# Attention fills: the score products of two slots issued together, in turns over four strips of 32 rows

## The chip, the core and the metric

One core of a Trainium2 chip runs the whole program. TensorE (PE) multiplies, VectorE (DVE) and ScalarE (ACT) read its results from PSUM, GpSimd (POOL) masks and issues indirect DMAs, SyncE (SP) issues the other DMAs. The metric is the device time of the kernel in microseconds, the median of several runs. Everything is float32; the profile shows each float32 product as two passes on PE (two weight loads and two matmuls).

## The reference

The input x has 8 batches of 512 rows and 128 columns. Three blocks follow one another: half a feed-forward block with a top-2 mixture of 8 experts, causal attention with 16 heads of 8 columns, and the same feed-forward block again. Only attention is touched here:

```
q = (x @ q_w + q_b)  -> 16 heads of 8 columns          k, v likewise from kv_w
att = q @ k.T / sqrt(8) + slope[h] * (key - query)     (512 x 512 for each batch and head)
att = where(key <= query, att, -inf); att = softmax(att)
y = att @ v, heads joined, @ o_w + o_b
x = x + y            (x here is layer-normalised on the way in)
```

## The kernel before

Attention works in **units**: one batch b and a group g of 4 heads, so 8 x 4 = 32 units. The four heads of a unit lie in four strips of 32 partitions (rows 32j to 32j+31) of the tiles `qs` and `ks`, and head j of a product uses strip j of PE's rows alone. A strip holds the head's 8 columns and some constant rows for the position term and the causal mask. One row of `qs` (`R_MAX`) holds, for each query, the maximum of its scores.

Each unit makes every score twice.

- `fill_a` makes scores with the queries on the partitions (`sa`). DVE reads them (line 925) and keeps the maximum of each query in `mx`. A unit has 12 fills f: f // 4 picks a pack of query tiles, `PACKS_A`, and f % 4 the head. The packs make products of 128 and 256 columns, of 384, and of 512.
- `maxima` transposes `mx` on PE (`pm`), copies it with ACT (`mr`) and sends it with four DMAs on SP's queue into the rows `R_MAX` of `qs`, one DMA for each head.
- `fill_b` makes the scores again with the keys on the partitions (`sb`), now with the maximum taken off by the row `R_MAX`. ACT takes the exponential into `pr` (line 964), and on each fourth fill POOL sets the masked corner of four heads to zero (line 969). Its packs make products of 512 columns, of 384, and of 256 and 128. The head is (f + 2) % 4.
- `weigh` multiplies the probabilities with v (`py`, three parts), `leave` copies the sum with ACT, `divide` transposes it on PE (`pyt`) and DVE divides by the sum of the row.

Time is cut into **slots**. Slot s issues one fill of each pass: `fill_a` number s and `fill_b` number s - LAG, where LAG is 20. With s % 4 = c the first uses strip c and the second strip (c + 2) % 4. Fills of `sa` have three PSUM buffers (`ps_a`), those of `sb` three others (`ps_b`), and everything else two (`ps_x`, tag "misc").

Behind the fills of a slot stand its **tasks**, from the dictionary `todo`. With r for the slot within a unit of 12 slots, the tasks that use PE are: r = 1 `py` part 1, r = 2 `pm`, r = 4 `py` part 2 and `leave`, r = 6 `pyt`, r = 10 `py` part 0. Once in a batch come, for the batch after or before: in the second unit `turn` (`apt`, r = 11); in the third `spread` (`pp`, r = 3 and 5), `turn_back` (`pyT`, r = 8), `project` (`apo`, r = 9), `f_stats` (r = 10, on DVE and ACT) and `values` (`pv`, r = 11); in the fourth `f_turn` (`pt`, r = 3), `f_half` (r = 5, ACT) and `f_logits` (`pl`, r = 6). In the first two batches the tasks also fetch and mix what the experts of the block before made, and after the fourth batch `f_sort` and `f_send` sort rows for the block after.

Matrix products, transposes and some POOL and ACT instructions keep the order in which the program issues them (`mm`, `tp`, `pin`). The others are ordered for each engine by a planner, which goes by data, by program order and by its own times. [...]

The loop that sets the order of a slot is this:

```
            for s in range(max(todo) + 1):
                if 0 <= s < UNITS * FILLS:
                    fill_a(*divmod(s, FILLS))
                if 0 <= s - LAG < UNITS * FILLS:
                    fill_b(*divmod(s - LAG, FILLS))
                for f, args in todo.get(s, ()):
                    f(*args)
```

Of the kernel before, what the change touches and what calls it, by code (L numbers as in the profile page):

```python
# [56 lines left out]
def tile_macaron(  # L57
# [125 lines left out]
    def mm(*args, **kw):  # L183
        pin(T.matmul(*args, **kw))  # L184
# [699 lines left out]
    def attention():  # L884
# [4 lines left out]
        with ExitStack() as ph:  # L889
# [13 lines left out]
            FILLS = 3 * GH  # L903
            LAG = FILLS + 8
            UNITS = NB * NG


            def fill_a(u, f):
                b, g = divmod(u, NG)
                pack, j = PACKS_A[f // GH], f % GH  # L910
                if f == 0:
                    mxs[u] = two.tile([P, GH, TT], F32, name=f"mx{u}", tag="mx")
                q, k, r = qs[b % 2], ks[b % 2], slice(32 * j, 32 * j + 32)
                sa = ps_a.tile([P, S], F32, name=f"sa{u}_{f}", tag="sa")
                at = 0
                for i in pack:
                    n = (i + 1) * P
                    mm(
                        sa[:, at : at + n], q[r, g, i * P : n], k[r, g, :n], start=True, stop=True
                    )  # L920
                    at += n
                at = 0
                for i in pack:
                    n = (i + 1) * P
                    V.tensor_tensor_reduce(  # L925
                        junk[:, :n], sa[:, at : at + n], mask_q[:, S - n :],
                        1.0, -3.0e38, ALU.add, ALU.max, mxs[u][:, j, i : i + 1],
                    )
                    at += n
# [16 lines left out]
            def fill_b(u, f):  # L946
                b, g = divmod(u, NG)
                p, j = f // GH, (f + 2) % GH
                pack = PACKS_B[p]
                width = sum(S - kt * P for kt in pack)  # L950
                if f % GH == 0:
                    prs[u, p] = prob.tile([P, GH, width], F32, name=f"pr{u}_{p}", tag=f"pr{p}")
                pr = prs[u, p]
                q, k, r = qs[b % 2], ks[b % 2], slice(32 * j, 32 * j + 32)
                sb = ps_b.tile([P, S], F32, name=f"sb{u}_{f}", tag="sb")
                at = 0
                for kt in pack:
                    n = S - kt * P
                    mm(
                        sb[:, at : at + n], k[r, g, kt * P : (kt + 1) * P], q[r, g, kt * P :],  # L960
                        start=True, stop=True,
                    )
                    at += n
                A.activation(pr[:, j, :], sb[:, :width], AF.Exp)  # L964
                if f % GH == GH - 1:
                    at = 0
                    for kt in pack:

                        pin(G.affine_select(  # L969
                            out=pr[:, :, at : at + P], in_=pr[:, :, at : at + P],  # L970
                            pattern=[[0, GH], [1, P]], compare_op=ALU.is_ge, fill=0.0,
                            base=0, channel_multiplier=-1,
                        ))
                        at += S - kt * P
# [54 lines left out]
            todo = {}  # L1029

            def at(slot, f, *args):
                todo.setdefault(slot, []).append((f, args))
# [18 lines left out]
            for u in range(UNITS):  # L1051
                s = u * FILLS
# [7 lines left out]
                if u % NG == NG - 1:  # L1060
# [11 lines left out]
                    if b == GROUP - 1:  # L1072
                        at(done + 24, f_sort, 1, 0, ps_x)
                        for k in range(GROUP * TT):
                            at(done + 28 + 3 * k, f_send, 1, *divmod(k, TT))
            for s in range(max(todo) + 1):
                if 0 <= s < UNITS * FILLS:
                    fill_a(*divmod(s, FILLS))
                if 0 <= s - LAG < UNITS * FILLS:
                    fill_b(*divmod(s - LAG, FILLS))  # L1080
                for f, args in todo.get(s, ()):
                    f(*args)

    def between(psum):

# [9 lines left out]
    constants()  # L1095
    f_first(between)
    attention()
    f_second()

# [81 lines left out]
```

## Time and profile before

| what | value |
|---|---|
| median of 3 runs | 1014.27 us (1010.85 to 1017.79) |
| the profiled execution, its own time | 1012.17 us |
| its span from the first to the last instruction | 1010.1 us |
| granted TensorE clock, mean over the span | 0.86 |
| PE, DVE, ACT, POOL busy | 800.7, 546.6, 446.9, 348.7 us |
| attention: start of the first `sa` product to start of the last `sb` product | from 287.5 to 787.3 us of the span |
| products of `sa` and of `sb`, passes | 1024 and 1024 |
| reads of `sa` by DVE (line 925) | 512, mean 490 ns |
| exponentials by ACT (line 964) | 384, mean 524 ns |

Attention is half of the span. The page's row of the granted clock is in tenths of full speed for 40 equal slices. In a timeline a row has its start in us from the start of the span, how long it took, the engine, the line, the operation, output <- inputs, and behind x how many instructions are merged in the row. Matrix products all have line 184, transposes line 187, since helpers issue them. A matmul's row covers the time until its last result, so rows of matmuls overlap; the time that PE needs is read from the start of one to the start of what follows it.

### The profile page before, as it was taken

Reading aid. Unit: us, or ns where it says so; the run is one execution under the profiler, and the core shown is the slowest. Engines: PE = TensorE matmul, PEld = TensorE weight load, DVE = VectorE, ACT = ScalarE, POOL = GpSimd, SP = SyncE. Lnnn points to the kernel's source line nnn. Section 1 sums busy time; section 2 is a strip of 40 time slices with the busy share of each in tenths; the row PEclk is TensorE's granted clock in tenths of the full one; section 3 lists DMA queues with packets and bytes.
Section 4 is the critical chain, followed back from the end, with each engine's and each line's share of the span. In section 5 each row is a group of like instructions: output and inputs, shape, how many; then the busy total and the mean of one; then the engine's idle time right before and its main releaser. Section 6 shows DMA issues by size and latency. Waiting matters only on the chain.

```text
span 1010.1 us, 17346 instructions
## 1 busy us (share of the span) xinstructions
PE 800.7 (79%) x5546; PEld 554.1 (55%) x5546; DVE 546.6 (54%) x2049; ACT 446.9 (44%) x928; POOL 348.7 (35%) x421
## 2 busy tenths in 40 slices
PE   4569888767668689999999967999999779956800
PEld 4469777656545345555555533455655578845800
DVE  5855533254338565676767672676773253445323
ACT  2434233235203355767676732666766434412300
POOL 4277700245034521121212138332111047074075
PEclk9579989978766777999999975999999789978955
DMA  9973166756621300101010101201000346766622
GB/s 259 299 188 75 56 224 221 217 158 178 159 71 25 69 14 11 36 4 43 4 44 3 44 17 49 56 10 42 4 3 2 107 148 217 248 178 179 218 58 68
DMA packets 104010, 101.22 MB, mean 100 GB/s; under 512 B 11424, under 2 KB 80936, under 8 KB 103640
## 3 DMA queue, kind: packets, MB, share of 16 engines
q1 hardware_dynamic: 95728, 83.26, 28.5%
q0 software_dynamic: 8192, 16.86, 6.0%
q8 instruction: 44, 0.72, 0.3%
q14 instruction: 46, 0.38, 0.1%
HBM read 34.37 MB, written 32.89 MB: 67 GB/s over the span
## 4 chain that ended last, share of the span: by engine, by line
PE 65%; DMA 8%; issue 7%; POOL 7%; DVE 7%; SPq 3%; ACT 2%; POOLq 0%; DVEq 0%; ACTq 0%
PE sa L184 18%; PE sb L184 9%; PE py L184 8%; POOL ye L599 6%; PE ph L184 6%; PE po L184 6%; DMA ye<-yd,to 4%; DMA xr<-xd 3%; PE rp L184 3%; PE pl L184 2%; PE pyt L187 2%; PE px L187 2%; PE pp L184 2%; SPq L509 1%; PE ab L184 1%
## 5 line engine op out<-in xcount | busy, mean ns | idle before, releaser
L925 DVE CUSTOM_DVE_ANT_0 junk<-sa,mask_q 128x128 f32<-128x128 f32 (+3 forms) x512 | 251.1, 490 | 146.1 <-PE sb L184 96.4
L184 PE MATMUL sa<-ks,qs 32*128 32x128 f32 (+3 forms) x1024 | 289.9, 514 | 15.4 <-DVE mx L925 15.2
L184 PE MATMUL sb<-qs,ks 32*128 32x256 f32 (+3 forms) x1024 | 284.8, 502 | 5.5 <-DMA qs<-mr 5.5
L964 ACT ACTIVATE pr<-sb 128x384 f32<-128x384 f32 (+1 forms) x384 | 188.6, 524 | 153.9 <-PE sb L184 142.7
L599 POOL DMA_INDIRECT ye<-yd,to x128 | 123.1, 961 | 239.5 <-DMA r<-rec 68.9
L184 PEld LDWEIGHTS sa<-ks,qs 32*128 32x128 f32 x1024 | 126.6, 203 | 117.8 <-DVE mx L925 88.4
L969 POOL TENSOR_SCALAR_AFFINE_SELECT pr<-pr 128x512 f32<-128x512 f32 x128 | 80.0, 637 | 302.5 <-ACT pr L964 302.4
L468 POOL DMA_INDIRECT xd<-xh,to x128 | 125.3, 979 | 110.3 <-issue 34.6
L546 ACT ACTIVATE hs<-ph,r 128x256 f32<-128x256 f32 x184 | 82.7, 474 | 151.9 <-PE ph L184 143.4
L184 PEld LDWEIGHTS sb<-qs,ks 32*128 32x128 f32 x1024 | 136.1, 199 | 18.3 <-issue 8.1
L184 PE MATMUL ph<-xs,r 128*128 128x256 f32 x368 | 113.5, 438 | 38.2 <-issue 24.4
L184 PEld LDWEIGHTS po<-r,hs 128*128 128x128 f32 x736 | 105.2, 208 | 6.0
L184 PE MATMUL po<-r,hs 128*128 128x129 f32 x736 | 104.5, 290 | 0.0
L184 PEld LDWEIGHTS ph<-xs,r 128*128 128x128 f32 x368 | 74.1, 224 | 48.4 <-issue 40.1
L184 PE MATMUL py<-pr,va 128*32 128x512 f32 (+3 forms) x1024 | 94.8, 469 | 2.8 <-POOL pr L969 2.8
L561 DVE TENSOR_TENSOR y<-po,r 128x258 f32<-128x258 f32 x92 | 39.0, 424 | 80.3 <-PE po L184 65.9
L532 DVE TENSOR_SCALAR xs<-px,cs 128x256 f32<-128x256 f32 x92 | 49.6, 541 | 53.9 <-PE px L187 51.5
L613 DVE TENSOR_TENSOR ye<-ye,wts 128x516 f32<-128x516 f32 x32 | 22.0, 696 | 91.2 <-DMA ye<-yd,to 91.2
L187 PE MATMUL px<-ident,xr 128*128 128x128 f32 x184 | 40.7, 308 | 38.0 <-DMA xr<-xd 32.3
L620 ACT ACTIVATE gt<-gt,half_gcb 128x4 f32<-128x4 f32 x16 | 4.7, 296 | 114.9 <-DVE gt L619 114.9
L184 PEld LDWEIGHTS py<-pr,va 128*32 128x32 f32 x1024 | 24.4, 112 | 53.9 <-issue 23.0
L187 PEld LDWEIGHTS px<-ident,xr 128*128 128x128 f32 x184 | 24.1, 156 | 50.2 <-issue 31.8
(185 smaller groups left out, 850.2 us busy)
## 6 DMA issues: line engine op xcount, KB each, us to landing
r<-rec SPq DMA_DIRECT2D x92, 322.5 KB
yd<-y SPq DMA_DIRECT2D x92, 129.0 KB
xr<-xd SPq DMA_DIRECT2D x92, 128.0 KB
xd<-blank SPq DMA_DIRECT2D x2, 2944.0 KB
qkd<-qk SPq DMA_DIRECT2D x16, 256.0 KB
x<-in_x_dram SPq DMA_DIRECT2D x8, 256.0 KB
qs<-in_alibi_q_dram SPq DMA_DIRECT2D x2, 1024.0 KB
ks<-in_alibi_k_dram SPq DMA_DIRECT2D x2, 1024.0 KB
```

What stands on the lines that cost most here:

```text
L184: pin(T.matmul(*args, **kw))
L187: pin(T.transpose(*args))
L468: d = G.indirect_dma_start(out=xd[g], out_offset=bass.IndirectOffsetOnAxis(to[:, k, j : j + 1], 0), in_=xhs_f[n, b][:, t, :], in_offset=None,)
L509: e = nc.sync.value_load(whose[0:1, t : t + 1], min_val=0, max_val=NE - 1)
L532: V.tensor_scalar(xT, pt.rearrange("p c q -> p (c q)"), cs[:, C_GAMMA : C_GAMMA + 1], cs[:, C_BETA : C_BETA + 1], ALU.mult, ALU.add,)
L546: A.activation(got[t][3][:, c, :], ph[:, :SLOTS], AF.Gelu, bias=r[:, E_B1 + c : E_B1 + c + 1])
L561: V.tensor_tensor(y, po, r[:, E_B2:RECORD].unsqueeze(1).to_broadcast([P, CHUNKS, PO]), ALU.add)
L599: pin(G.indirect_dma_start(out=back[b][k][:, t, :], out_offset=None, in_=yd[g], in_offset=bass.IndirectOffsetOnAxis(to[:, k, j : j + 1], 0),))
L613: V.tensor_tensor(ys[k], ys[k], wts[:, k, js].unsqueeze(2).to_broadcast([P, TT, PO]), ALU.mult)
L925: V.tensor_tensor_reduce(junk[:, :n], sa[:, at : at + n], mask_q[:, S - n :], 1.0, -3.0e38, ALU.add, ALU.max, mxs[u][:, j, i : i + 1],)
L964: A.activation(pr[:, j, :], sb[:, :width], AF.Exp)
L969: pin(G.affine_select(out=pr[:, :, at : at + P], in_=pr[:, :, at : at + P], pattern=[[0, GH], [1, P]], compare_op=ALU.is_ge, fill=0.0, bas ...
```

## The change

Two slots are now one step. The two fill functions become generators that yield behind each product. For slots s and s + 1 the four fills are put into the order `fill_a` of s, `fill_b` of s, `fill_b` of s + 1, `fill_a` of s + 1, and one product is taken from each in turn until all are done. These four use the four strips. The tasks of slot s and then those of s + 1 follow behind all four fills. Before, the tasks of slot s stood ahead of the fills of slot s + 1. The number of products, reads and exponentials and the number of PSUM buffers stay as they were.

```diff
@@ fill_a
                         sa[:, at : at + n], q[r, g, i * P : n], k[r, g, :n], start=True, stop=True
                     )
                     at += n
+                    yield
@@ fill_b
                         start=True, stop=True,
                     )
                     at += n
+                    yield
                 A.activation(pr[:, j, :], sb[:, :width], AF.Exp)
@@ attention
-            for s in range(max(todo) + 1):
-                if 0 <= s < UNITS * FILLS:
-                    fill_a(*divmod(s, FILLS))
-                if 0 <= s - LAG < UNITS * FILLS:
-                    fill_b(*divmod(s - LAG, FILLS))
-                for f, args in todo.get(s, ()):
-                    f(*args)
+            for s in range(0, max(todo) + 1, 2):
+                fills = []
+                for i in (0, 1):
+                    if 0 <= s - LAG < UNITS * FILLS:
+                        fills.append(fill_b(*divmod(s + i - LAG, FILLS)))
+                    if 0 <= s < UNITS * FILLS:
+                        fills.insert(3 * i, fill_a(*divmod(s + i, FILLS)))
+                while fills:
+                    fills = [f for f in fills if next(f, fills) is not fills]
+                for i in (0, 1):
+                    for f, args in todo.get(s + i, ()):
+                        f(*args)
```

## The prediction

> **What bounds the kernel now.** I read the page first: the slices by engine and the chain of work that ended last.
>
> ```profile
> PE   4569888767668689999999967999999779956800
> PEclk9579989978766777999999975999999789978955
> PE 65%; DMA 8%; issue 7%; POOL 7%; DVE 7%; SPq 3%; ACT 2%; POOLq 0%; DVEq 0%; ACTq 0%
> ```
>
> PE carries the chain, and in attention (slices 12 to 31) it is full, at full clock, but for two dips. The stage table says the same for one full stretch and one dip:
>
> ```profile
> 500.00:550.00 50.00, 50.00 (x424) 27.72 (x422) 34.17 (x146) 34.54 (x73) 10.43 (x16) 1.00 0.10 23
> 580.00:630.00 50.00, 35.44 (x243) 18.88 (x233) 24.99 (x110) 16.20 (x37) 27.79 (x32) 0.68 0.08 32
> ```
>
> PE "busy 50 of 50" does not yet mean that PE is the limit, for a row of a matmul covers its latency. So I went to the waits from 400 to 550 us:
>
> ```profile
> ACT pr L964 <- PE sb L184: 40.3, 63, 1.5
> DVE junk L925 <- PE sb L184: 29.8, 37, 1.3
> PEld sa L184 <- DVE mx L925: 25.2, 47, 0.8
> ```
>
> Both sides wait: DVE for products, and PE, 47 times, for DVE's read that frees a buffer of `sa`. The limit changes from unit to unit. From `pm` to `pm` the four units of a batch take 17.6, 13.4, 10.8 and 11.5 us (starts at 505.50, 523.11, 536.47, 547.24, 558.72: 53.2 us). DVE's reads, start to start, cost 0.91 (128 + 256 columns), 0.71 (384) and 0.845 (512), so a unit's twelve and its division (0.27) need 4 x 2.465 + 0.27 = 10.13 us. The units of 10.8 and 11.5 are nearly DVE's; in that of 17.6 PE goes from one thing to the next.
>
> The timeline of that last one shows what four strips do already:
>
> ```profile
> 512.60 0.58 PE L184 MATMUL sa<-ks,qs 32*128 32x384 f32 x1
> 512.61 0.48 PE L184 MATMUL sb<-qs,ks 32*128 32x256 f32 x1
> 512.62 0.69 PE L184 MATMUL sa<-ks,qs 32*128 32x512 f32 x1
> 512.63 0.69 PE L184 MATMUL sb<-qs,ks 32*128 32x512 f32 x2
> ...
> 513.68 0.66 PE L187 MATMUL pyT<-ident,ys 128*128 128x128 f32 x4
> ...
> 514.26 0.69 PE L184 MATMUL sa<-ks,qs 32*128 32x512 f32 x1
> 514.27 0.69 PE L184 MATMUL sb<-qs,ks 32*128 32x512 f32 x1
> ...
> 514.47 0.59 ACT L1019 COPY yo<-pyT 128x512 f32<-128x512 f32 x1
> ...
> 515.32 1.16 PE L184 MATMUL apo<-ow,yo 128*128 128x128 f32 x8
> ```
>
> Slots 7 and 8 have no PE task between them: their four fills start within 0.03 us, and the next thing starts after 1.08 us. Slot 9, alone on two strips, takes 1.06. So **two adjacent slots run on four strips at the price of one**, before the change.
>
> **What the change does, then.** It adds no parallel work where slots already touch. Its work is to move the tasks of even slots behind the odd slot, so that runs of fills merge. No instruction goes or comes.
>
> A rule speaks against even that. The Trainium skill ("TensorE: Matmul & The Clock Gate", Part 3) states a measured 3.07-fold speed for four row strips, not 4. Against one strip that is 4 / 3.07 = 1.30 of its time for four; if two strips cost 1.0, a pair would cost 0.3 more, 24 pairs a batch 7 us, eight batches 56 us slower. The row says 1.08 against 1.06. I take the row: about nothing.
>
> **Gain on PE alone.** A run costs 0.85 (one slot of 384 columns, 522.26 to 523.11) to 0.87 (two, 520.61 to 521.48), with 512 columns 1.06 to 1.08.
> - Third unit: the runs {0,1}{2}{3}{4}{5}{6}{7,8}{9}{10}{11} become six pairs: 2 x 0.85 + 2 x 1.06 = 3.8 us saved.
> - Fourth: {2}{3} merge, 0.85. {4}{5,6} become {4,5}{6,7}: nothing.
> - Second: {11} joins the run of 8 to 10: 1.06. First: none.
>
> Together 5.7 us a batch, 46 us over eight. That is the ceiling.
>
> **What is late next.**
>
> *Buffers.* A pair needs two buffers of `sa`, and the second fill waits until DVE has read slot s - 2. The page's rule (same part) is that matmuls start in strict order. The trace is looser once they are issued (at 512.63 an `sb` starts before the second pass of the `sa` ahead of it), but a product that waits for a semaphore does hold what is issued behind it. By the rule the second product of the first fill waits behind the blocked last one; by the row it might slip through, for at most 0.2 us earlier, and the pair's end is the same. I take the rule.
>
> First unit by hand, t = 0 at slot 0, DVE still busy until 0.45: pair (0,1) readable at 0.95; reads until 1.86 and 2.77; `py` part 1 until 1.73; `sa` of slot 3 waits for 1.86, so (2,3) ends 2.75. `pm`. `sa` of slot 5 waits for read 2 (3.7), ends 4.7; `py` part 2 until 5.4; (6,7) readable at 6.4, DVE idle since 6.0; `pyt` until 6.9. `sb` of slot 9 needs its row `R_MAX`: 4.54 behind `pm` now (536.47 to 541.01), so 7.3, and the last `sa` stands behind it. `sa` of slot 11 waits for read 8 (8.95), ends 10.0; `py` part 0 until 11.0. DVE has 0.45 left: the state repeats. **11.0 against 10.77: +0.25.** Second unit, with `apt` (0.6): 11.6 against 11.5, +0.1. Where DVE is the limit the old spread of the tasks fed it a little better.
>
> *Queues passed.* Moved tasks take their DMAs along. `maxima` sends four, one slot later: priced above. `spread` sends five (nine with the zero rows), used 19 slots later or more: covered. A fetch or send on POOL at an even slot may come behind one mask (0.64), and the mask's reader `weigh` stands 7 slots behind: covered.
>
> *Tasks that now stand side by side.* `pm` and `pp` (or `pt`) share two "misc" buffers with the sum `py`, so the second needs ACT's copy of the first:
>
> ```profile
> 505.50 0.28 PE L187 MATMUL pm<-ident,mx 128*16 128x128 f32 x1
> 505.51 0.86 ACT L964 ACTIVATE pr<-sb 128x384 f32<-128x384 f32 x2
> ...
> 506.25 0.24 ACT L937 COPY mr<-pm 16x128 f32<-16x128 f32 x1
> ...
> 506.56 0.30 PEld L184 LDWEIGHTS pp<-hT,qk_c 128*128 128x128 f32 x2 [0.33 <-ACT mr L937]
> ```
>
> The copy stands behind two exponentials. Today slot 3 runs in this wait and PE loses 0.33. After the change slot 3 is already done: PE idles some 0.75. In the third unit `pp` then ends at 4.77 from slot 0 (before: 4.62): the merged run of 0.85 is lost. So with `pyT` and `apo`: today slot 9 covers ACT's copy `yo`; afterwards the copy waits for two exponentials (1.15) and takes 0.6, against a `pyT` of 0.6, and about 1.1 is lost of 1.06 saved.
>
> Third unit, summed: (0,1) 0.88, `py` 0.78, (2,3) to 2.75, `pp` to 4.77, (4,5) 5.63, `py` 6.42, `pp` 7.48, (6,7) 8.33, `pyt` 8.95, (8,9) 10.02, `pyT` (waits for the division) 10.75, `apo` 11.85 to 12.95, (10,11) 14.02, `py` 15.0, `pv` 16.1. Before 17.62: 1.5 saved.
>
> *Then ACT gives it back.* `f_stats` needs `project`, then DVE's statistics, a table load (1.28), two roots, a table load, and `f_norm` (1.64), before the exponential of slot 0 may run; slot 3's `sb` needs that one's buffer. With both reads of (10,11) ahead of the statistics I get them done at 16.8 (before: 16.1), and the exponential of slot 0 done at 20.8; before it was 20.9. So the 1.5 goes into waiting. Then `pm`, copy, `pt` at 22.5 against 21.8, and carried on with the same steps, `py` part 1 of the next first unit comes 0.44 later than before.
>
> **Sum:** 0.44 + 0.25 + 0.1 = +0.8 us a batch, eight batches +6.4: 1018.6 beside the profiled execution's 1012.2. The median lies 2.1 above that execution: **1020 us**.
>
> The dips (290 to 385, 582 to 625) I cost at nothing, for lack of a nearer row. There DVE stands in line behind rows of the experts, and SP makes 23 loads of tile numbers (line 509) ahead of `qs<-mr`, for which PE waited 5.5 us. The planner may place these otherwise: below, all 5.5 gone, -6; above, the same again in each dip, +11.
>
> **Rivals.**
> - **Faster, 993 us.** PE keeps what it saves: the planner puts the statistics ahead of the two reads, ACT's chain starts 1.0 to 1.5 earlier, and the third unit keeps 1.5, the fourth 0.85, the second 0.3: 2.65 a batch, 21 in all. For it: PE's gapless third unit. Against: the buffer shared by `pm`, `pp` and `pt`, and DVE's 10.13 of 10.8.
> - **Slower, 1036 us: the third buffer.** The wait of the pair's last `sa` for read s - 2 now holds the tasks of both slots. DVE's other work in a batch (division 4 x 0.27, `va` 0.88, statistics and their small steps 2, the `project` sum 0.7, `lg` 0.2: near 5) slips ahead of such a read wherever the planner likes. If 2.8 of it reach PE in each batch, 22 us. It decides once PE's wait for line 925 from 400 to 550 exceeds some 40 us instead of 25.
> - **Strips interfere:** +56 by the rule above, 1070. The row makes this under 0.02; it is in the slower case.
>
> **Chances and range.** Measurements of this kernel tell 1% (10 us) from nothing. Near nothing (1020) 0.40, faster 0.25, slower 0.35. For the most likely case alone the range is 1008 to 1032, its sum with the dips. The 8-in-10 range must reach into both rivals: 994 to 1042.
>
> **What would show it.** Right: PE still full in attention, units of some 11.0 and 11.6; third unit shorter by 1 to 2, fourth longer in part; new waits of PE for ACT (`mr` ahead of `pp` and `pt`, `yo` ahead of `apo`); products of `sa` and `sb` as long as before. Wrong: a third and fourth unit together under 29 us (before 31), or a first unit under 10.5 (faster); a first unit over 11.5 with `sa` waiting for line 925 (slower); 512-column passes over 0.7 at full clock (strips interfere).

## The result and the profile after

The changed kernel takes 1049.93 us (median of 4 runs, 1045.26 to 1052.66) beside 1012.56 for the kernel before (4 runs, one more than ahead of the prediction): a ratio of 1.0367, 95% interval 1.0294 to 1.044. It is slower by 37 us. The forecast was 1020, the range ended at 1042. The profiled execution took 1045.26, its span 1043.4 (before 1010.1). Attention went from 500.1 to 534.6; what lies ahead of it from 287.5 to 289.0, what lies behind it from 222.5 to 219.8. So the loss is in attention alone (its end is taken here as the end of the last `sb` product). Ratios leave slowed executions out, and two of the profiles below are of slowed ones: those of the statistics moved by a slot, 13 us (even pairs) and 10 us (odd pairs) above the median of their kernel.

First the slices and the granted clock, as shown of before:

```profile
PE   5569787676678778998989867899898779955900
PEclk8579989879866889898989885989698989987955
```

But for two dips, slices 12 to 31 were nines in PE and in its clock. Now both fall below nine again and again, and mostly together. The stage rows for the same two stretches as before (us, then busy time of PE, weight loads, DVE, ACT, POOL with counts, then the clock):

```profile
500.00:550.00 50.00, 44.82 (x379) 23.30 (x375) 30.16 (x129) 32.98 (x68) 9.35 (x14) 0.90 0.10 24
580.00:630.00 50.00, 35.31 (x246) 18.31 (x246) 28.11 (x126) 23.32 (x47) 15.56 (x19) 0.77 0.11 28
```

In the stretch that was full (PE 50.00, clock 1.00) PE now stands idle for 5.2 of 50 us, and the clock is 0.90. The waits between 400 and 550 say for whom (us in total, times, longest):

```profile
PEld sa L184 <- DVE mx L926: 18.3, 34, 0.8
PEld sb L184 <- ACT pr L966: 16.7, 18, 3.1
PE sb L184 <- ACT pr L966: 7.5, 3, 2.5
DVE rs L307 <- ACT rs L306: 7.4, 3, 2.5
```

PE's weight loads wait less for DVE's reads than before (18.3 instead of 25.2). The new waits are for ACT: PE for exponentials, and DVE for a square root of `f_stats`, once in each of the three batches of this window and 2.5 us each time. Line 306 is the second root, line 305 the first.

From `pm` to `pm`, in batches that nothing else disturbs:

| us | third unit | fourth | first | second | batch |
|---|---|---|---|---|---|
| before | 17.61 | 13.35 | 10.77 | 11.48 | 53.2 |
| forecast | 16.1 to the same point, then given back: 31.4 together | | 11.0 | 11.6 | 54.0 |
| after | 20.0 to 20.7 | 15.0 to 15.7 | 10.75 | 11.36 | 57.4 to 57.8 |

First and second unit did not move. All of it, some 4.5 us a batch, is in the third and fourth unit. Seven batches run `f_stats` within attention. In these, third and fourth unit together lose 3.6 to 9.2 us, 36.1 in sum; attention as a whole loses 34.5.

Before, the roots stood side by side on ACT, between one load of their table and one of the exponential's:

```profile
518.23 1.28 ACT L305 ACT_TABLE_LOAD   x1
519.52 0.30 ACT L305 ACTIVATE rs<-mv,eps_c 128x4 f32<-128x4 f32 x1
519.72 0.28 ACT L306 ACTIVATE rs<-mv,eps_c 128x4 f32<-128x4 f32 x1
520.02 1.28 ACT L964 ACT_TABLE_LOAD   x1
```

The timeline after, at the place where DVE waited (start, us, engine, line, operation; idle before it in brackets):

```profile
525.88 0.60 ACT L966 ACTIVATE pr<-sb 128x512 f32<-128x512 f32 x1 [2.34 <-PE sa L184]
526.49 1.28 ACT L305 ACT_TABLE_LOAD   x1
527.79 0.30 ACT L305 ACTIVATE rs<-mv,eps_c 128x4 f32<-128x4 f32 x1
528.10 1.28 ACT L966 ACT_TABLE_LOAD   x1
529.39 0.60 ACT L966 ACTIVATE pr<-sb 128x512 f32<-128x512 f32 x1
530.01 1.28 ACT L306 ACT_TABLE_LOAD   x1
531.30 0.30 ACT L306 ACTIVATE rs<-mv,eps_c 128x4 f32<-128x4 f32 x1
531.62 1.28 ACT L966 ACT_TABLE_LOAD   x1
...
533.46 1.00 PE L184 MATMUL sb<-qs,ks 32*128 32x384 f32 x1 [2.50 <-ACT pr L966]
...
536.24 1.11 PE L187 MATMUL pt<-ident,xh 128*128 128x128 f32 x4 [0.82 <-ACT mr L938]
```

Read it from the top. The exponential of slot 10 ends, a table is loaded, the first root runs. Then the table of the exponential is loaded again, the exponential of **slot 11** runs, and the table of the root is loaded a second time for the second root. Four loads where before there were two: there the roots start 0.20 us apart; here they are 3.51 us apart. Over the whole kernel ACT has 14 instructions more (942 for 928), two loads in each of seven batches; in attention 31 loads for 17. The last two lines show what follows. PE has waited 2.50 us, and its passes then take 1.00 us for 384 columns (0.58 before) and 1.11 for the transposes of `pt` (0.66 before) until about 542: the granted clock is at half, from 0.75 us into this wait on (the last section has the rows).

### The profile page after: what moved, and what is told of

It is laid out like the page before. It is cut to its first block, busy times and chain, and to the rows that moved or that the text cites. A ratio compares the mean times of both kernels' runs of the same rounds, so it can differ in the third digit from the quotient of the medians.

```text
span 1043.4 us, 17358 instructions
## 1 busy us (share of the span) xinstructions
PE 791.9 (76%) x5546; PEld 525.3 (50%) x5546; DVE 543.9 (52%) x2049; ACT 457.5 (44%) x942; POOL 347.9 (33%) x421
## 5 line engine op out<-in xcount | busy, mean ns | idle before, releaser
L184 PE MATMUL sa<-ks,qs 32*128 32x128 f32 (+3 forms) x1024 | 273.9, 542 | 19.8 <-DVE mx L926 19.8
L184 PE MATMUL sb<-qs,ks 32*128 32x512 f32 (+3 forms) x1024 | 251.7, 525 | 26.1 <-ACT pr L966 20.4
L966 ACT ACTIVATE pr<-sb 128x384 f32<-128x384 f32 (+1 forms) x384 | 182.2, 523 | 155.3 <-PE sa L184 110.5
L184 PEld LDWEIGHTS sa<-ks,qs 32*128 32x128 f32 x1024 | 116.7, 214 | 103.9 <-DVE mx L926 82.3
L184 PEld LDWEIGHTS sb<-qs,ks 32*128 32x128 f32 x1024 | 115.1, 212 | 69.0 <-ACT pr L966 52.4
L184 PE MATMUL ph<-xs,r 128*128 128x256 f32 x368 | 110.0, 427 | 39.5 <-issue 25.3
L184 PE MATMUL py<-pr,va 128*32 128x512 f32 (+3 forms) x1024 | 98.2, 486 | 5.7 <-POOL pr L971 5.7
L184 PEld LDWEIGHTS ph<-xs,r 128*128 128x128 f32 x368 | 71.5, 216 | 49.5 <-issue 41.7
L532 DVE TENSOR_SCALAR xs<-px,cs 128x256 f32<-128x256 f32 x92 | 49.6, 540 | 57.3 <-PE px L187 57.3
```

Of the source, the lines that this page charges most:

```text
L532: V.tensor_scalar(xT, pt.rearrange("p c q -> p (c q)"), cs[:, C_GAMMA : C_GAMMA + 1], cs[:, C_BETA : C_BETA + 1], ALU.mult, ALU.add,)
```

## The theories

- **Tables.** In the new order `f_stats` (r = 10, the statistics) stands behind the fills of r = 10 and 11 and so behind both exponentials. The planner, which orders ACT by its own times, sets the exponential of slot 11 between the two roots. Two more table loads, a longer wait of PE, and the half clock that begins in it make the loss.
- **Chain.** The pair (2,3) needs the buffer of `sb` that the exponential of slot 0 frees, and that one stands behind the roots and `f_norm`. What PE saves in the third unit is waited for there. This is the prediction's own step.
- **Neighbours.** Tasks that need one another's results now stand side by side: the waits of `pp` and `pt` for `mr`, and of `apo` for `yo`, cost it.
- **Turns.** Alternating products over four strips costs something by itself.

Two groups of runs fell on chips where the kernel before itself takes 1147.4 and 1143.8 us (354 to 365 us ahead of attention instead of 287.5), so a ratio is read only beside its own runs of before. The units of an undisturbed batch have nearly the same lengths wherever a kernel was profiled on two chips, and most readings rest on them. All runs at a glance ("loads": table loads in attention):

| kernel | third, fourth unit | batch | loads | ratio to before |
|---|---|---|---|---|
| before | 17.61, 13.35 | 53.2 | 17 | |
| after | 20.0-20.7, 15.0-15.7 | 57.4-57.8 | 31 | 1.0367 [1.0294, 1.044] |
| after, again | 20.0-20.2, 15.0-15.8 | 57.3-57.8 | 31 | 1.0213 [1.0167, 1.0259] |
| no turns | 19.6-20.3, 15.0-15.7 | 57.3-57.8 | 31 | 1.022 [1.0155, 1.0285] |
| before, one root | 17.61, 13.07 | 52.9 | 17 | 0.996 [0.9935, 0.9985] |
| after, one root | 18.96, 13.5 | 54.6 | 17 | 1.0132 [1.0051, 1.0213] |
| before, roots split | 20.2-20.4, 16.7-19.2 | 59.2-62 | 31 | 1.0414 [1.0369, 1.0459] |
| after, statistics a slot earlier | 18.64, 13.60 | 54.3 | 17 | 1.0114 [1.0081, 1.0147] |
| after, neighbours apart | 14.73, 17.66 | 54.5 | 17 | 1.0061 [1.0035, 1.0087] |
| after, chain earlier | 19.13, 13.5 (once 19.4) | 54.7 (once 60.6) | 17 | 1.0128 [1.0055, 1.0201] |
| odd pairs | 16.02, 12.70 | 50.95 | 17 | 0.9898 [0.9822, 0.9974] |
| odd pairs, again | 16.03, 12.69 | 50.95 | 17 | 0.9899 [0.9845, 0.9953] |
| odd pairs, ln and exp | 16.12, 12.73 | 51.1 | 17 | 0.9885 [0.9835, 0.9934] |
| odd pairs, statistics a slot later | 15.83, 19.49 | 57.5 | 31 | 1.0175 [1.0094, 1.0256] |

The changed kernel itself cost 37 us on one chip and 24 to 26 on another, while its undisturbed batches took the same 57.3 to 57.8 us on both. Why the rest differs stays open.

## Experiments

**The change again, and the turns alone.** In the second kernel each fill is issued whole, in the same order of fills:

```diff
-                while fills:
-                    fills = [f for f in fills if next(f, fills) is not fills]
+                for f in fills:
+                    for _ in f:
+                        pass
```

> The changed kernel as it is, as a base for the others of this series. Ratio to the kernel before 1.03 to 1.04; per batch (from pm of a first unit to the next, undisturbed batches) 57.5 to 58 us against 53.2.

> The changed kernel without the turns: the four fills of a step are issued whole, one behind the other, in the same order (fill_a of s, fill_b of s, fill_b of s + 1, fill_a of s + 1). Tables: the planner sees the same steps, 1043 to 1052. Theory I (turns): the second product of a fill that waits behind the blocked last fill makes the loss; then 1012 to 1025.

The batch repeats on another chip (57.3 to 57.8); the ratio, 1.0213, is below the 1.03 to 1.04 expected. Without turns it is the same, with the same 31 loads. So the turns do nothing that shows, neither good nor bad; "turns" falls. What acts is that the tasks of the even slot stand behind the odd slot.

**The roots in one instruction, in both kernels.** The two arguments are made by DVE, and one activation takes all roots, so nothing can come between them:

```diff
-        A.activation(rs[:, 0, :], mv[:, :, 1], AF.Sqrt, bias=eps_c)
-        A.activation(rs[:, 1, :], mv[:, :, 1], AF.Sqrt, bias=eps2_c, scale=1.0 + EPS)
+        V.tensor_scalar(rs[:, 0, :], mv[:, :, 1], EPS, None, ALU.add)
+        V.tensor_scalar(rs[:, 1, :], mv[:, :, 1], 1.0 + EPS, EPS * EPS, ALU.mult, ALU.add)
+        A.activation(rs, rs, AF.Sqrt)
```

> The changed kernel, but f_stats takes both roots in one instruction on ScalarE (two small steps on VectorE make the two arguments first), so that no exponential can stand between them. Theory T (tables): in the changed kernel the planner puts the exponential of slot 11 between the two roots, which costs two more table loads of 1.28 us in each of 7 batches, 18 us, and through the idle PE a halved clock in the fourth unit; without it 1015 to 1022 us, ACTIVATE table loads back to 14 in attention, third unit near 17, fourth near 13.4. Theory M (merging): the tasks that moved, their waits for ScalarE and for buffers make the 37 us; then still 1042 to 1050.

> The kernel before with the same single root. Both theories: no exponential stood between the roots here, so 1006 to 1016 us, not to be told from the kernel before. It is the base for the changed kernel with one root.

The loads fall from 31 to 17 and the batch from 57.6 to 54.6. The same edit takes 0.3 from the kernel before, so 2.7 of the 3.0 come from the roots being together. What stays, 54.6 against 52.9, is 1.7 us a batch. The ratio, 1.0132, is above what was expected. In the profile of this kernel the last three units took 60.2 us (37.3 + 22.9), in that of the other one-root kernel 41.0 (27.6 + 13.4): here the granted clock stood at half for 47.8 us up to the end of attention.

**The roots split in the kernel before.** An exponential of one column is pinned between the two roots in the seven batches; nothing else changes:

```diff
+            pin(A.activation(rs[:, 0, :], mv[:, :, 1], AF.Sqrt, bias=eps_c))
+            pin(A.activation(dummy2, dummy, AF.Exp))
+            pin(A.activation(rs[:, 1, :], mv[:, :, 1], AF.Sqrt, bias=eps2_c, scale=1.0 + EPS))
```

> The kernel before with one thing of the changed kernel alone: in the f_stats of the seven batches inside attention an exponential of one column on ScalarE stands between the two roots, kept in that order, which costs two more table loads (2.57 us). It is additional work, and its result is not used. Theory T (tables): the ScalarE chain is on the path to the next units, so third and fourth unit together grow by 2.5 to 4.5 us from 31, ratio 1.015 to 1.03. Theory M (merging): the loss in the changed kernel has another cause and the kernel before hides ScalarE: under 1 us a batch, ratio under 1.007.

Its timeline has the same pattern, with the pinned exponential at line 310:

```profile
545.73 1.28 ACT L310 ACT_TABLE_LOAD   x1
547.03 0.20 ACT L310 ACTIVATE dummy<-dummy 128x1 f32<-128x1 f32 x1
547.24 1.28 ACT L311 ACT_TABLE_LOAD   x1
...
550.79 0.91 PE L187 MATMUL sb<-qs,ks 32*128 32x384 f32 x2 [1.70 <-ACT pr L972]
```

The split alone makes the kernel before slower by 4.1%, 6 to 9 us a batch. That is more than was expected, and more than the 2 x 1.28 + 0.2 of what was put in: the rest comes after it, as a fourth unit of 16.7 to 19.2 us with `pt` at 1.11 us, the half clock again. (The pins also fix the order among these three and other pinned instructions, so a little of it may be theirs.) Here the Trainium skill ("ScalarE: Activation LUTs", section "Table sets: the hidden batching unit") has the rule: keep activations of one table set together, since a change of set has to load a table. Its price (section "What ACT_TABLE_LOAD costs") is 1.28 us and a drain of 1.38. The rows show 1.28 and a next instruction 0.01 to 0.02 later, with no room for a drain. Two extra switches are 2.6 us by the row and 5.3 by the page; the trace's row holds, and what comes on top of it shows on PE.

**The place of the statistics.** One number of the changed kernel:

```diff
-                    at(done + 14, f_stats, 1, (b,))
+                    at(done + 13, f_stats, 1, (b,))
```

> One number of the changed kernel is altered: f_stats (slot done + 14, r = 10) is issued at done + 13, so behind project but ahead of the fills of r = 10 and 11 instead of behind them. Nothing else moves; the roots stay two instructions. If the loss comes from where the statistics stand (behind the reads and exponentials of r = 10 and 11, so that the planner sets the exponential of slot 11 between the roots), then the table loads in attention fall from 31 to 17, a batch from 57.6 to 53 to 54.5 us, and the ratio to the kernel before is 0.995 to 1.015. If the statistics only go ahead of work that the planner orders by its own times anyway, nothing changes: 31 loads, 57.6 us, ratio 1.02 or more.

Now `f_stats` is issued ahead of the fills of r = 10 and 11, and ACT's timeline reads so:

```profile
518.59 0.30 ACT L305 ACTIVATE rs<-mv,eps_c 128x4 f32<-128x4 f32 x1
518.79 0.28 ACT L306 ACTIVATE rs<-mv,eps_c 128x4 f32<-128x4 f32 x1
519.09 1.28 ACT L966 ACT_TABLE_LOAD   x1
...
520.88 1.63 ACT L326 ACTIVATE xh<-x,nm,rs 128x128 f32<-128x128 f32 x4
522.42 1.23 ACT L966 ACTIVATE pr<-sb 128x384 f32<-128x384 f32 x3
...
522.94 0.58 PE L184 MATMUL sb<-qs,ks 32*128 32x384 f32 x1 [1.00 <-ACT pr L966]
```

The roots are 0.20 apart, with one load ahead of them and one behind: 17 loads in attention, 54.3 us a batch; 3.3 of the 4.5 us are gone with one number. The slot at which `f_stats` is issued decides it. (How the 3.3 divide between the two loads, the longer wait and the slower clock is not shown: a stretch at half clock is left here too, but of 3.4 us instead of 6.8 to 10.2 in the undisturbed batches.) The last line is the rest: the fill of slot 3 waits for the exponential of slot 0, which stands behind `xh`, the 1.63 us of `f_norm`. That is "chain".

**Neighbours apart, and the chain earlier.** Both with the roots in one instruction:

```diff
# neighbours apart
-                at(s + FILLS + 2, maxima, u)
+                at(s + FILLS + 1, maxima, u)
-                    at(done + 13, project, b)
-                    at(done + 14, f_stats, 1, (b,))
+                    at(done + 14, project, b)
+                    at(done + 15, f_stats, 1, (b,))
# chain earlier
-                    at(done + 12, turn_back, b)
-                    at(done + 13, project, b)
-                    at(done + 14, f_stats, 1, (b,))
+                    at(done + 11, turn_back, b)
+                    at(done + 12, project, b)
+                    at(done + 13, f_stats, 1, (b,))
```

> The changed kernel with the single root, and three tasks moved so that those which wait for one another stand in different steps: maxima one slot earlier (a step ahead of pp and pt), project and f_stats one slot later (a step behind pyT). With the single root alone a batch took 54.6 us, 1.6 over the kernel before. If the waits of neighbours for ScalarE (pm before pp and pt, pyT before apo) are the rest, the batch takes 51.5 to 53 us, ratio 0.99 to 1.0. If the rest is in the buffers (the pair's last sa waiting for the read of slot s - 2), it stays at 54 to 55, ratio 1.01.

> The changed kernel with the two roots of f_stats in one ACT instruction, and with turn_back, project and f_stats each one slot earlier (done + 11, 12 and 13), so that each falls into the step ahead: turn_back beside divide, then project and f_stats together, ahead of the fills of r = 10 and 11. If the chain from project over the roots to the exponential of slot 0 sets the third and fourth unit together, a start of one step earlier takes 1.5 to 3 us off the 54.55 us that a batch takes with one root alone: 51.5 to 53 us, 17 loads, ratio 0.985 to 1.0. If instead the waits of PE beside its neighbours (division ahead of turn_back, the copy yo ahead of apo) set it, what is won is lost there: a batch stays at 54 to 55 us, ratio 1.005 to 1.015.

With the neighbours apart the third unit falls from 18.96 to 14.73 and the fourth rises from 13.5 to 17.66: the sum, 32.4, is what it was. PE no longer waits for `yo`, but `pm` stands before the pair (2,3) now, and its copy `mr` behind ACT's chain, and `pt` waits for it:

```profile
550.17 1.11 PE L187 MATMUL pt<-ident,xh 128*128 128x128 f32 x4 [3.76 <-ACT mr L939]
```

So with even pairs "neighbours" falls as the cause of the rest: their waits are real, but without them the time goes to the next wait for the same chain. The earlier chain was to show "chain" from the other side, and it missed: 54.7 instead of 51.5 to 53 (and one batch of 60.6, with the clock at half for 17 us), with this order on ACT:

```profile
519.21 0.21 ACT L307 ACTIVATE rs<-rs 128x8 f32<-128x8 f32 x1
519.89 1.65 ACT L327 ACTIVATE xh<-x,nm,rs 128x128 f32<-128x128 f32 x4 [0.47 <-DVE nm L309]
521.55 1.28 ACT L967 ACT_TABLE_LOAD   x1
...
523.39 0.58 PE L184 MATMUL sb<-qs,ks 32*128 32x384 f32 x1 [2.05 <-ACT pr L967]
```

The exponentials of slots 10 and 11 came ahead of the roots, and the load for the next ones comes behind `xh`, so the exponential of slot 0 starts at 522.85 and PE waits 2.05 us for it. The kernel with one root alone has this very order and a wait of 2.06 at the same place. So a third order of ACT's list exists that keeps the roots together and still holds PE up, and an earlier start of the chain alone did not shorten the wait; that PE's earlier waits (`pyT` for the division, 1.35 us) took up the start is likely, but not tried by itself.

**Odd pairs.** The steps start one slot earlier, so that slots pair as (11,0), (1,2), (3,4) ...; then `f_stats` one slot later in that kernel; and odd pairs with the roots as logarithm and exponential:

```diff
-            for s in range(0, max(todo) + 1, 2):
+            for s in range(-1, max(todo) + 1, 2):
-                    if 0 <= s - LAG < UNITS * FILLS:
+                    if 0 <= s + i - LAG < UNITS * FILLS:
-                    if 0 <= s < UNITS * FILLS:
+                    if 0 <= s + i < UNITS * FILLS:
# statistics a slot later, besides
-                    at(done + 14, f_stats, 1, (b,))
+                    at(done + 15, f_stats, 1, (b,))
# ln and exp, besides, without "a slot later" (the one root of the first normalisation in attention likewise)
-        A.activation(rs[:, 0, :], mv[:, :, 1], AF.Sqrt, bias=eps_c)
-        A.activation(rs[:, 1, :], mv[:, :, 1], AF.Sqrt, bias=eps2_c, scale=1.0 + EPS)
-        V.reciprocal(rs, rs)
+        A.activation(rs[:, 0, :], mv[:, :, 1], AF.Ln, bias=eps_c)
+        A.activation(rs[:, 1, :], mv[:, :, 1], AF.Ln, bias=eps2_c, scale=1.0 + EPS)
+        A.activation(rs, rs, AF.Exp, scale=-0.5)
```

> The changed kernel with the steps one slot earlier: pairs (11,0), (1,2), (3,4) and so on instead of (0,1), (2,3). Then pm and pp (or pt), and pyT and apo, stand in different steps again, and f_stats stands a step ahead of slot 11. Tables: no exponential of slot 11 can be due between the roots, 1005 to 1020. Merging: only the waits for ScalarE between neighbours go (about 25 us of PE's waits in the trace), 1022 to 1030.

> The pairs (11,0), (1,2), (3,4) ... once more, in five rounds, for a closer interval of the fastest version so far. Expected 0.985 to 0.995 of the kernel before, a batch at 51 us, 17 loads. If its first result was chance, 1.0 within the interval.

> The pairs (11,0), (1,2) ... as in the kernel with odd pairs, but f_stats one slot later (done + 15, r = 11), so that it is issued behind the fills of r = 11 and 0 instead of ahead of them; nothing else differs. If the place of the statistics in the order is what decides, the loss of the even pairs comes back: roots apart again, 31 table loads in attention, a batch 53 to 56 us instead of 50.95, ratio 1.0 to 1.03. If the pairs (11,0) are faster because tasks that wait for one another are no longer neighbours, a batch stays within 0.5 us of 50.95 and the ratio near 0.99.

> The changed kernel with the steps one slot earlier (pairs (11,0), (1,2) and so on), and with the normalisations' 1 / sqrt(v) made as exp(-0.5 ln(v)) on ScalarE in place of root and reciprocal. If logarithm and exponential come from one table, attention needs no table load for f_stats: 2.57 us less of ScalarE in the chain of the third unit, a batch 49 to 50.5 us against 51, ratio 0.975 to 0.985. If they come from two tables, the loads stay or double: ratio 0.99 or above 1.

Odd pairs are faster than the kernel before, by 1%: 0.9898 and, on another chip in more rounds, 1001.51 us beside 1010.82, 0.9899 [0.9845, 0.9953]. The four units are 16.03, 12.69, 11.11 and 11.1. Now the third unit keeps what PE saves, and the wait for ACT is short:

```profile
509.67 0.28 ACT L306 ACTIVATE rs<-mv,eps_c 128x4 f32<-128x4 f32 x1
...
511.26 0.98 ACT L966 ACTIVATE pr<-sb 128x512 f32<-128x512 f32 x2
...
511.91 0.58 PE L184 MATMUL sb<-qs,ks 32*128 32x384 f32 x1 [0.54 <-ACT pr L966]
```

After the roots the exponentials of slots 10 and 11 come first, and the pair (1,2) needs only these two; slot 0's, behind `xh`, is needed by the pair (3,4), a step later and behind `pm`. That is the chain with a step of slack, as the order of the rows shows it. It is not parted from "neighbours" here: with odd pairs the matmuls of `pp` wait 0.34 for `mr` (0.88 with even pairs), and those of `pt` and, in undisturbed batches, of `apo` no longer wait for ACT. The same kernel with `f_stats` one slot later is the mirror of the experiment before: 31 loads again, a fourth unit of 19.49 for 12.69, a batch of 57.5 (53 to 56 was expected), 1.0175 for 0.99. By the place of one small task the same pairing is 1% faster or 1.7% slower. Ln and exp gained nothing over odd pairs: 17 loads as before, and a batch of 51.1 for 50.95. In its rows the logarithm and the exponential each had a load of 1.28 us in front.

## Why the prediction was wrong

- **The step that failed is "Then ACT gives it back".** It took "a table load (1.28), two roots, a table load" as one block, as it stood in the profile before, although the change put `f_stats` behind the exponentials that compete with it. The block was split: four loads. The step had the exponential of slot 0 done at 20.8 from slot 0 of the unit and `pt` at 22.5; in the trace (slot 0 at 511.60) they are at 21.8 and 24.6, and the fourth unit then ran in part at half clock. Sized: 3.3 us a batch, by what moving `f_stats` gave back, about 23 us in seven batches, where the forecast had nothing.
- **What that step did have was there, and small.** Without the split the third and fourth unit lose 18.64 + 13.60 - 30.96 = 1.3 us (forecast 0.44), and the batch 1.1 (forecast 0.8; that these come so close is luck, since the first two units were off the other way). The saving in the third unit did turn into the wait of slot 3's `sb`. Both terms together, 7 x (3.3 + 1.3) = 32, and the one batch that lost 9.2 us instead of some 4.6, make up the 36 us that the third and fourth units lost.
- **The third unit by hand holds to 0.2 us.** `pp` ended at 4.77 by hand and 4.96 in the trace, the second `pp` at 7.48 and 7.66, `apo` at 12.95 and 13.08, `pv` at 16.1 and 16.24. The two waits it added are there:

```profile
515.51 0.30 PEld L184 LDWEIGHTS pp<-hT,qk_c 128*128 128x128 f32 x2 [1.07 <-ACT mr L938]
...
523.59 0.97 PEld L184 LDWEIGHTS apo<-ow,yo 128*128 128x128 f32 x8 [1.13 <-ACT yo L1021]
```

- **First and second unit** were to lose 0.25 and 0.1; they gained 0.02 and 0.12. The hand sums were too slow by 0.27 and 0.22.
- **The dips**, costed at nothing: the first took 88.55 us for 90.73, the second, with one batch's loss in it, 85.50 for 80.27. PE's wait for `qs<-mr` is 5.3 for 5.5. Costing them at nothing was near enough.
- **Faster, 993.** Its condition came true in part: the statistics went between the two reads, and were done at 15.8 where my sum had 16.8. It did not help, because ACT's chain came apart behind them. With odd pairs something like its mechanism appears, 2.2 us a batch where it had 2.65.
- **Slower, the third buffer.** At 1036 it came nearest, by luck, for its reason did not occur: PE's wait for the read fell from 25.2 to 18.3, where it was to exceed 40.
- **Strips interfere** fell: 512-column passes are 0.59 to 0.69 at full clock, and issuing the fills without turns changed nothing.
- **The range** was made of terms for which a row of before stood. (Its inner part, 1008 to 1032, is called a sum with the dips; -6 and +11 about 1020 give 1014 to 1031.) A term for "the planner orders ACT otherwise" was in neither end, though the text said that the planner may place things as it likes for DVE.

## What to carry to other kernels

When an edit moves work in the program's order, list what the scheduler may now slip between two activations that share a table, and price it as two more loads plus the wait behind them; better, make the pair one instruction or issue it ahead of its competitors. When work is issued in groups over a ring of buffers, check for each group which release it needs last, and choose the phase of the grouping so that the slowest release has a whole group of slack. And a wait of PE of a few microseconds can cost more than itself: look at the durations of the passes behind it.

## What was not expected of the hardware

PE's clock fell to half within attention although PE was busy for most of the time. By the stage rows of 520 to 550 us, then of the 3.4 us ahead of the fall at 531.71 and of the stretch behind it:

```profile
520.00:550.00 30.00, 25.70 (x199) 13.66 (x194) 17.05 (x73) 20.30 (x40) 4.34 (x7) 0.83 0.14 28
528.30:531.70 3.40, 2.57 (x22) 0.81 (x14) 0.89 (x6) 3.34 (x5) 0.63 (x1) 1.00 0.25 33
531.72:541.94 10.22, 7.67 (x54) 4.75 (x54) 3.88 (x22) 7.59 (x17) 0.63 (x1) 0.50 0.01 2
```

This is the kernel after, 0.83; in the same 30 us it is 1.00 before, 1.00 with odd pairs and 0.94 with the statistics a slot earlier. The wait of 2.50 us ran from 530.96 to 533.46, so the clock fell 0.75 us into it, and the full length of this wait cannot be the reason; in the 3.4 us up to the fall PE's rows cover 2.57. It came back 10.24 us later. All ten half stretches of this kernel between 400 and 823 us are whole multiples of 3.41 us: 6.83 (three), 10.24 (five), 13.65 and 20.48 (the batch that lost 9.2 us). The Trainium skill ("TensorE: Matmul & The Clock Gate", Part 1) describes a clock that is either half or full, and goes back to half after an idle window of about 3.4 us. Half or full, and the 3.4, are what these rows show; that the window must be idle is not, with PE at 2.57 of 3.40. The way back is not a matter of a few busy microseconds either. In the changed kernel with one root, at the end of attention, the clock stayed at half for 47.8 us:

```profile
849.28:897.06 47.78, 46.02 (x225) 20.77 (x229) 8.20 (x31) 17.65 (x39) 6.86 (x11) 0.50 0.00 1
```

PE's rows cover 46.02 of it (a row includes latency, so PE may have worked less). How busy PE must be for the clock to hold, or to come back, stays open.
